# Start, first chunk and tail of a fused attention and convolution kernel: constant matmuls, a later spread, and another order of the last loads

## The chip, the cores and the metric

The kernel runs on one core of a Trainium2 chip. The time is device time in microseconds (us), median over several executions. A profile is one execution recorded by the hardware profiler; its span is the time from the first to the last recorded work. Engines are named as the profile names them: PE (TensorE, matmul), PEld (its weight load), DVE (VectorE), ACT (ScalarE), POOL (GpSimd) and SP (SyncE, which only starts transfers here). Each engine works through its own list of instructions in the order in which the program wrote them.

## What is computed

Two images, each of 256 channels and 64 x 64 pixels, all in float32, go through two layers.

Layer 0 is attention over all 4096 pixels of an image, with 8 heads of 32 channels, mixed with the input by a mask:

```python
attn = jax.nn.softmax(jnp.einsum('bnd,bmd->bnm', q, k), axis=-1)
fuse = jnp.einsum('bnm,bmd->bnd', attn, v)
hybrid = _conv1x1(jnp.concatenate([x, fuse], axis=1), Wf, bf)
return hybrid * m + x * (1.0 - m)
```

Layer 1 scales each channel by a gate made of two small matmuls, adds a second attention inside windows of 8 x 8 pixels (4 heads of 64 channels), shuffles the channels, runs two grouped 7 x 7 convolutions with normalisation between them, and returns the result times the sigmoid of the second convolution:

```python
y = lax.conv_general_dilated(x, sa_w1, (1, 1), [(3, 3), (3, 3)], dimension_numbers=dn, feature_group_count=cr)
y = jax.nn.relu(_bn(y + sa_b1))
y = lax.conv_general_dilated(y, sa_w2, (1, 1), [(3, 3), (3, 3)], dimension_numbers=dn, feature_group_count=cr)
return x * jax.nn.sigmoid(_bn(y + sa_b2))
```

## The kernel before

**Opening.** The pixels of an image are cut into 8 chunks of 512. For each of the 16 chunks of both images the kernel makes q and k (line 435, 16 matmul records to a chunk), then v (line 472), and writes them to memory outside the core. ACT starts the loads of the three weight matrices and then sixteen small loads of the biases `bq` and `bk` (lines 383 and 392) before its first arithmetic, the copy with bias at line 445. The squares of q and k go to DVE (line 454), whose maxima decide later between two versions of the attention; line 415 sums them by head on PE. The version that runs here is called `a`.

**Attention.** `pipeline` runs over 1024 slots: image `b`, chunk `c` of queries, half `g` of the heads (4 heads), block `m` of 128 keys. A chunk has 64 slots. In slot i, `scores(i + 2)` puts the score matmuls (line 633) on PE and three exponentials (line 643) on ACT, `products(i)` puts the value matmuls (line 662) on PE and, except at m = 0, one addition of 128 x 2048 elements on DVE (line 664), which sums the exponentials for the denominators. The exponentials lie in `EB = 8` buffers, so those of slot i + 8 can be written once the addition of slot i is done.

When a chunk's last slot is done, `at(delay, action)` puts actions into a list; an action runs at the end of the slot that is `delay` later. With `DN = 8`: after 8 slots the denominators are gathered on PE (line 685), after 9 DVE takes reciprocals (line 714), after 10 and 12 `spread` puts four matmuls each on PE (line 700) that spread the reciprocals over the channels, after 13 DVE multiplies the attention result `f` by them (line 717), and after 14 `stage(b, c)` is appended to the list of stages (line 1188).

A stage is everything of a chunk that follows its attention: the 1 x 1 convolution (line 732; first the half on `x`, then the half on `f`), the gate (lines 761 and 775), the window attention (lines 803 to 931) and its output projection (line 953). It is a generator cut into steps; every fourth slot runs one step (`run_stages`), so that its work lies among the slots of the next chunk. Its last step writes the chunk's rows, via `xo`, to the array `x_s` outside the core (line 979). Its first step also starts, on SP, the loads of the next chunk's `x` and mask (`load_x`, lines 573 and 576), which wait until this chunk's are no longer needed.

**Tail.** The convolutions start when the attention ends. They work on units of 4 groups of channels: 16 units, with both images wherever that is possible. `items` lists the work: the first `EARLY` units with image 0 alone, whose rows are complete; units 2 to `EARLY` - 1 with image 1 alone; the remaining units with both images; and last units 1 and 0 with image 1. `convolve` is a generator too. Its steps are `conv1(k + 1)` (line 1045), `conv2(k)` (line 1069) and `gate(k)` (lines 1091 and 1104, the last multiplication and the stores), and after each gate come the loads that the coming items need. These loads are started on SP, in program order with half of the stores: `load_rows` (line 1024) brings the pixels of item k + 4, `load_w` (line 1017) a unit's convolution weights of 896 KB. Weights of units other than 0 go into the 8 buffers that held exponentials. Two of them are loaded when the tail starts, one more after each gate.

While the last chunk's stage still runs, one step of `convolve` is placed after each of its larger steps. When it is done, `staged` is set; from then on `more()` makes the buffers for the rows of image 1 and loads the first four of them (`load_rows(EARLY + 3)`), which waits for the last chunk's rows to have arrived in `x_s`. The gates of the early items after that store through POOL alone.

Of the kernel before, what the change touches and what calls it, by code (L numbers as in the profile page):

```python
# [19 lines left out]
P = 128  # L20
# [9 lines left out]
AHEAD = 2  # L30
EB = 8
DN = 8
EARLY = 8
HEADS1, HD1 = 4, 64
WS = 8
NW = W // WS
# [19 lines left out]
def conv_seq_kernel(ctx: ExitStack, tc: tile.TileContext, a, out):  # L56
    nc = tc.nc
# [13 lines left out]
    def psum2(name):  # L71
        return ps["pair"].tile([P, 2, CH], F32, tag="s", name=name)

    def psum1(name):
        return ps["one"].tile([P, CH], F32, tag="h", name=name)
# [6 lines left out]
    ones = const.tile([P, P], F32, name="ones")  # L82
# [249 lines left out]
    def spread(row, n):  # L332
        f = row.shape[-1]
        return row.rearrange("p u f -> u p f").to_broadcast([NU, n, f])
# [37 lines left out]
    with (  # L372
# [38 lines left out]
        def norms(i, tops):  # L411
# [3 lines left out]
                nc.tensor.matmul(s_, headsum, tops[:, n, :], start=True, stop=True)  # L415
            nc.vector.tensor_reduce(nm[:, i : i + 1], s[:, 0 : CH // 4], AX.X, ALU.max)

        prepared = prepare(mk, cwp)
        next(prepared)
        for _ in range(3):  # L420
# [2 lines left out]
        for i, (b, c) in enumerate(chunks):  # L423
# [4 lines left out]
            for n, w in (("q", wq), ("k", wk)):  # L428
                s = psum2(f"{n}0_{b}_{c}")
                for g in range(KC):  # L430
                    for kc in range(KC):
                        rhs = x[:, kc, :]
                        if n == "q":
# [5 lines left out]
                            start=(kc == 0),  # L439
                            stop=(kc == KC - 1),  # L440
# [26 lines left out]
        for i, (b, c) in enumerate(chunks):  # L467
            s = psum2(f"v0_{b}_{c}")
            sv = s.rearrange("p a (t o) -> p (a t) o", t=2)
            for m in range(4):  # L470
                for kc in range(KC):
# [4 lines left out]
                        start=(kc == 0),  # L476
                        stop=(kc == KC - 1),
# [21 lines left out]
            elif i == 2:  # L499
# [3 lines left out]
                for oc in range(KC):  # L503
                    for kc in range(KC):
# [4 lines left out]
                            start=(kc == 0),  # L509
                            stop=(kc == KC - 1),  # L510
# [13 lines left out]
    def pipeline(arm, shifted, pools):  # L524
# [23 lines left out]
        stages = deque()  # L548

        def at(delay, action):  # L550
            later.append((now[0] + delay, action))
# [99 lines left out]
        def products(i):  # L651
            b, c, g, m = slots[i]
            if m == 0:
                acc[0] = avp.tile([P, CH], F32, tag="av", name=f"av{arm}_{i}")
                acc[1] = ep.tile([P, HG, CH], F32, tag="sum", name=f"sum{arm}_{i}", bufs=3)
                totals[b, c, g] = acc[1]
            av, total = acc[0], acc[1]
            e, v = es[i], vts[b, c, g, m // PB]
            start, stop = m == 0, m == NMB - 1
            for j in range(HG):  # L660
                r = slice(32 * j, 32 * j + 32)
                nc.tensor.matmul(av[r, :], v[:, m % PB, r], e[:, j, :], start=start, stop=stop)  # L662
            if m > 0:
                nc.vector.tensor_add(total, first[0] if m == 1 else total, e)  # L664
            e = es.pop(i)
            if start:
                first[0] = e
            if stop:
                if g == 0:
                    fts[b, c] = fp.tile([P, KC, CH], F32, tag="f", name=f"f{arm}_{b}_{c}")  # L670
                f = fts[b, c]
                nc.scalar.copy(f[:, g, :], av)  # L672
                if g == 0:
                    return
                both = [totals.pop((b, c, gg)) for gg in range(KC)]
                inv = fp.tile([P, P], F32, tag="inv", name=f"inv{arm}_{i}")
                rd = fp.tile([P, KC, 4, P], F32, tag="rd", name=f"rd{arm}_{i}")


                def denominators():  # L680
                    s = psum2(f"dn{arm}_{i}")
                    for h in range(HEADS0):
                        for q in range(4):
                            r = slice(32 * q, 32 * q + 32)
                            nc.tensor.matmul(  # L685
                                s[r, 0, 0:P],
                                keysum[:, h].rearrange("p i h -> p (i h)"),
                                both[h // HG][:, h % HG, q * P : (q + 1) * P],
                                start=(h == 0),
                                stop=(h == HEADS0 - 1),  # L690
                            )
                    nc.scalar.copy(inv, s[:, 0, 0:P])


                def spread(hh):
                    t = psum2(f"rd{arm}_{i}_{hh}")
                    for gg in range(KC):
                        for q in range(2):
                            r = slice(64 * hh + 32 * q, 64 * hh + 32 * q + 32)
                            nc.tensor.matmul(  # L700
                                t[:, q, gg * P : gg * P + P],
                                spread_h[r, gg].rearrange("p j d -> p (j d)"),
                                inv[r, :],
                                start=True,
                                stop=True,
                            )
                    nc.scalar.copy(
                        rd[:, :, 2 * hh : 2 * hh + 2, :],
                        t[:, :, 0 : KC * P].rearrange("p q (g n) -> p g q n", g=KC),
                    )  # L710


                at(DN, denominators)
                at(DN + 1, lambda: nc.vector.reciprocal(inv, inv))
                at(DN + 2, lambda: spread(0))
                at(DN + 4, lambda: spread(1))
                at(DN + 5, lambda: nc.vector.tensor_mul(f, f, rd.rearrange("p g q n -> p g (q n)")))

# [266 lines left out]

        items = [(u, (0,)) for u in range(EARLY)] + [(u, (1,)) for u in range(2, EARLY)]
        items += [(u, (0, 1)) for u in range(EARLY, NU)] + [(1, (1,)), (0, (1,))]
        staged = []  # L990

        def convolve():
# [12 lines left out]
            weights = deque([*range(1, NU), 1])  # L1005
            dst = out.rearrange("b (g i) r w -> b i r g w", i=4)

            def load_w(u):
                if u >= NU:
                    return  # L1010
                n = 2 * 32 * UW
                if u == 0:
                    t = cpool.tile([P, n], F32, name=f"w{arm}{u}")
                else:
                    t = ep.tile([P, HG, CH], F32, tag="e", name=f"w{arm}{u}")
                    t = t.rearrange("p h n -> p (h n)")[:, 0:n]
                nc.sync.dma_start(t, w_s[u])
                ws[u] = t

            def load_x(k):  # L1020
                u, images = items[k]
                x = xs[k] = early[k % 4] if k < EARLY else xcs[k % 4]
                for i, b in enumerate(images):
# [5 lines left out]
            def load_rows(k):  # L1029

                while len(xs) < min(k + 1, len(items)) and (
                    staged or B - 1 not in items[len(xs)][1]
                ):
                    load_x(len(xs))
# [53 lines left out]
            def gate(k, z):  # L1088
# [5 lines left out]
                if k == len(items) - 1:  # L1094
                    engines = (nc.scalar, nc.sync)
                elif staged and k < EARLY:
                    engines = (nc.gpsimd,)
# [12 lines left out]
            def more():  # L1110
                if staged and not xcs:
# [5 lines left out]
                    xcs.append(pool.tile([P, B * nb, UG, WP], F32, name=f"xl{arm}3"))  # L1117
                    load_rows(EARLY + 3)
                return bool(xcs)
# [2 lines left out]
            load_rows(3)  # L1122
            load_w(0)
            pool = yield
            for _ in range(2):
                load_w(weights.popleft())
            conv1(0)
            yield
            for k, (u, images) in enumerate(items):
                while len(xs) <= k + 1 < len(items):  # L1130
                    if not more():
                        yield
                conv1(k + 1)
                yield
                more()
                z = conv2(k)
                yield
                more()
                gate(k, z)
                if xcs or k + 4 < EARLY:  # L1140
                    load_rows(k + 4)

                if weights and (k < EARLY - 1 or k >= EARLY):
                    load_w(weights.popleft())

        def run_later():
# [23 lines left out]
        for i, (b, c, g, m) in enumerate(slots):  # L1170
            now[0] = i
            if (b, c, g, m) == (B - 1, NCHUNK - 1, 0, 0):
                for _ in banded:
                    pass
                conv = convolve()
                next(conv)
            if m % PB == 0:
                load_piece(i // PB + AHEAD)
            if g == KC - 1 and m == 0:
                nxt = (b, c + 1) if c + 1 < NCHUNK else (b + 1, 0)  # L1180
                if nxt[0] < B:
                    load_q(*nxt)
            rest = scores(i + 2) if i + 2 < len(slots) else None
            products(i)
            if rest:
                rest()
            if g == KC - 1 and m == NMB - 1:
                at(DN + 6, lambda b=b, c=c: stages.append(stage(b, c)))
            run_later()
            if i % 5 == 1:  # L1190
                next(banded, None)
            if i % 4 == 0:
                run_stages()
# [102 lines left out]
```

## Time and profile before

| | |
|---|---|
| three executions | 3018.35, 3022.46 and 3022.87 us; median 3022.46 us |
| profiled execution | 3021.93 us |
| its span | 3020.1 us |
| PE busy | 2970.8 us, 98% of the span |
| DVE busy | 2503.1 us, 83% |
| ACT busy | 2480.6 us, 82% |
| POOL busy | 267.1 us, 9% |
| opening, to the first score matmul | 0 to 187.4 us |
| attention, to the last value matmul | 187.4 to 2781.5 us |
| tail | 2781.5 to 3020.1 us |

The profile gives each engine's busy time, a timeline of instructions in order of time, the waits, and the chain of work that ended last, followed back from the last instruction. In the timeline a row has its start, its length, the engine, the line and the operation; rows that follow each other closely are merged, with their number behind an x. Brackets at the end say how long the engine had been idle before the row, and what ended that. "SPq", "ACTq" and "POOL ... DMA" rows are starts of transfers, not the transfers themselves. In the chain a row has its start, its length, and the engine and line or the transfer.

### The profile page before, as it was taken

What the parts mean: (1) busy time and instruction counts of PE and PEld (TensorE: products, weight loads), DVE (VectorE), ACT (ScalarE), POOL (GpSimd) and SP (SyncE); (2) the same over time, 40 slices, a digit from 0 to 9 for tenths busy, and PEclk for the clock granted to TensorE, in tenths of its full rate; (3) what the DMA queues carried; (4) which work ended last, traced back from release to release, by engine and by line L of the source; (5) the groups of instructions that cost most, each with busy time, mean ns of one, the idle gap of its engine ahead of it and who ended that gap; (6) DMA issues with size and microseconds to landing.
All of it is one profiled execution on the core that took longest, in us unless ns stands there. A gap on an engine that the chain in (4) does not pass through costs nothing.

```text
span 3020.1 us, 61026 instructions
## 1 busy us (share of the span) xinstructions
PE 2970.8 (98%) x25226; PEld 1017.2 (34%) x25226; DVE 2503.1 (83%) x1348; ACT 2480.6 (82%) x4151; POOL 267.1 (9%) x470
## 2 busy tenths in 40 slices
PE   9999899999999999999999999999999999999897
PEld 3552223223222222222223222323223222323585
DVE  3249989999999999998999999999999998998211
ACT  5569789898989898988989898989898998988333
POOL 8010000000000000000000000000000000000456
PEclk9999999999999999999999999999999999999998
DMA  8544322222142323232222222222323222321564
GB/s 243 196 174 160 107 69 66 69 65 70 52 80 63 79 62 73 66 73 68 67 68 64 71 58 67 62 73 62 80 59 69 71 71 67 104 60 54 163 196 104
DMA packets 224143, 266.03 MB, mean 88 GB/s; under 512 B 113576, under 2 KB 130300, under 8 KB 223600
## 3 DMA queue, kind: packets, MB, share of 16 engines
q1 hardware_dynamic: 200880, 231.47, 26.2%
q0 software_dynamic: 18416, 27.87, 4.4%
q8 instruction: 201, 3.29, 0.5%
q10 hardware_dynamic: 4560, 2.70, 0.3%
q14 instruction: 86, 0.70, 0.1%
HBM read 213.49 MB, written 66.13 MB: 93 GB/s over the span
## 4 chain that ended last, share of the span: by engine, by line
PE 92%; DVE 2%; DMA 2%; POOL 1%; ACT 1%; issue 1%; SPq 0%; ACTq 0%; DVEq 0%; POOLq 0%
PE sa L633 36%; PE ava L662 33%; PE hya L732 4%; PE qka L803 4%; PE vwa L889 2%; PE opa L953 2%; PE v L472 2%; PE q L435 2%; PE k L435 2%; DVE suma L664 1%; POOL out_dram L1104 1%; PE c1a L1045 1%; PE c2a L1069 1%; DMA out_dram<-za 1%; PE dna L685 1%
## 5 line engine op out<-in xcount | busy, mean ns | idle before, releaser
L664 DVE TENSOR_TENSOR suma<-suma,ea 128x2048 f32<-128x2048 f32 x960 | 2199.1, 2291 | 88.7 <-ACT ea L643 2.3
L643 ACT ACTIVATE ea<-sa 128x512 f32<-128x512 f32 (+1 forms) x3072 | 2044.8, 745 | 86.6 <-PE sa L633 39.3
L633 PE MATMUL sa<-qa,ka 32*128 32x512 f32 x8192 | 1191.4, 640 | 1.5 <-ACT vst L480 1.2
L662 PE MATMUL ava<-ea,va 128*32 128x512 f32 x8192 | 1091.6, 605 | 0.3 <-ACT fa L672 0.3
L633 PEld LDWEIGHTS sa<-qa,ka 32*128 32x128 f32 x8192 | 338.0, 183 | 755.4 <-ACT ea L643 688.3
L662 PEld LDWEIGHTS ava<-ea,va 128*32 128x32 f32 x8192 | 161.5, 108 | 779.7 <-issue 752.9
L979 POOL DMA_DIRECT2D xs<-xo x94 | 65.8, 708 | 2552.0 <-DVE xo L964 2551.8
L1104 POOL DMA_DIRECT2D out_dram<-za x210 | 117.9, 569 | 85.0 <-DVE za L1091 61.1
L803 PE MATMUL qka<-ua,qkv_w 128*128 128x512 f32 x256 | 118.4, 605 | 0.0
L664 DVE TENSOR_TENSOR suma<-ea,ea 128x2048 f32<-128x2048 f32 x32 | 73.1, 2284 | 51.3 <-ACT ea L643 51.3
L1091 DVE TENSOR_TENSOR za<-za,xla 128x768 f32<-128x768 f32 (+1 forms) x16 | 21.7, 1359 | 108.0 <-DMA out_dram<-za 57.9
L454 DVE TENSOR_REDUCE top<-sq 128x512 f32<-128x2048 f32 x16 | 36.6, 2286 | 81.3 <-ACT sq L448 81.3
L1069 PE MATMUL c2a<-yca,wa 32*128 32x192 f32 (+1 forms) x1344 | 98.1, 435 | 2.5 <-ACT za L1079 2.5
L740 ACT ACTIVATE ta<-hya,bf 128x512 f32<-128x512 f32 x32 | 20.2, 683 | 96.8 <-PE hya L732 96.8
L1079 ACT ACTIVATE za<-c2a 128x384 f32<-128x384 f32 (+1 forms) x48 | 26.1, 595 | 86.5 <-DMA out_dram<-za 61.4
L1069 PEld LDWEIGHTS c2a<-yca,wa 32*128 32x128 f32 x1344 | 89.6, 315 | 13.1 <-issue 9.8
L858 ACT ACTIVATE ewa<-ewa,mxwa 128x64 f32<-128x64 f32 x256 | 85.2, 346 | 1.5 <-DVE mxwa L849 1.5
L744 DVE TENSOR_TENSOR ta<-ta,mca 128x512 f32<-128x512 f32 x32 | 22.0, 689 | 67.6 <-ACT ta L740 67.6
L816 ACT ACTIVATE qka<-qka,qkv_b 128x512 f32<-128x512 f32 x64 | 40.4, 683 | 41.8 <-PE qka L803 41.6
L803 PEld LDWEIGHTS qka<-ua,qkv_w 128*128 128x128 f32 x256 | 46.0, 189 | 71.3 <-issue 46.1
L435 PE MATMUL q<-x,WqT 128*128 128x512 f32 x128 | 61.3, 624 | 5.6 <-DMA WqT<-in_WqT_dram 5.6
L889 PE MATMUL vwa<-qkv_w,ua 128*128 128x256 f32 x256 | 59.5, 386 | 0.0
(137 smaller groups left out, 1523.5 us busy)
## 6 DMA issues: line engine op xcount, KB each, us to landing
ka<-ks SPq DMA_DIRECT2D x256, 256.0 KB
va<-vs SPq DMA_DIRECT2D x256, 256.0 KB
wa<-ws SPq DMA_DIRECT2D x17, 896.0 KB
ws<-zeros SPq DMA_DIRECT2D x16, 896.0 KB
xs<-xo POOLq DMA_DIRECT2D x78, 140.0 KB, 5.8
xla<-xs SPq DMA_DIRECT2D x24, 420.0 KB
x<-in_x_dram SPq DMA_DIRECT2D x16, 512.0 KB
qs<-qst SPq DMA_DIRECT2D x16, 512.0 KB
```

The lines of the kernel that those rows point to most:

```text
L435: nc.tensor.matmul(s[:, g, :], w[:, kc, g * P : (g + 1) * P], rhs, start=(kc == 0), stop=(kc == KC - 1),)
L633: nc.tensor.matmul(heads[j], k[r, cols], q[r, g, :], start=True, stop=not shifted)
L643: nc.scalar.activation(e[:, h, :], tile, AF.Exp, scale=SCALE0)
L662: nc.tensor.matmul(av[r, :], v[:, m % PB, r], e[:, j, :], start=start, stop=stop)
L664: nc.vector.tensor_add(total, first[0] if m == 1 else total, e)
L732: nc.tensor.matmul(s[:, oc, :], wf[:, kc, oc * P : (oc + 1) * P], f[:, kc - KC, :] if half else xw[kc], start=(kc == 0), stop=(kc == 2 * K ...
L803: nc.tensor.matmul(s[:, j, :], wqkv[:, kc, o : o + P], u[:, kc, :], start=(kc == 0), stop=(kc == KC - 1),)
L858: nc.scalar.activation(e[:, n, :], e[:, n, :], AF.Exp, bias=mx[:, n : n + 1], accum_out=rs[:, n : n + 1],)
L889: nc.tensor.matmul(sv[:, t, :], u[:, kc, t * P : (t + 1) * P], wqkv[:, kc, 2 * C : 3 * C], start=(kc == 0), stop=(kc == KC - 1),)
L979: eng.dma_start(x_s[b, n, p + r0 : p + r1].rearrange("r g w -> g r w"), xo[64 * h : 64 * h + 64, oc, r0 - WS * c : r1 - WS * c, :],)
L1069: nc.tensor.matmul(tiles[j // 2][:, j % 2, 0 : n * W], w[r, d], y[r, 0:n, d : d + W], start=(d == 0), stop=(d == KS - 1),)
L1104: engines[stores % len(engines)].dma_start(dst[b, i, r0:r1, UG * u : UG * u + UG, :], z[p + r0 : p + r1, :, nb * m + n, :],)
```

## The change

Four edits.

1. Before the chunks' first matmuls, ten matmuls of a 128 x 128 tile of ones with itself, into a PSUM tile that nobody reads.
2. For the very first chunk alone, both spreads, the multiplication of `f` and the start of the stage come nine slots later than for the others (`late = EB + 1`). Denominators and reciprocals stay where they were.
3. Four units' weights are loaded when the tail starts, in place of two. After the gates, weights are loaded as long as the next unit is at most 9 (`1 + EB`), and then from item `EARLY` on. Before, one was loaded after each of the items 0 to 6 and from item 8 on.
4. `EARLY` is 7 in place of 8: unit 7 is done once for both images, not once for each. `items` has 23 entries where it had 24.

```diff
-EARLY = 8
+EARLY = 7
...
+        busy = psum1("busy")
+        for _ in range(10):
+            nc.tensor.matmul(busy[:, 0:P], ones, ones, start=True, stop=True)
...
+                late = EB + 1 if (b, c) == (0, 0) else 0
                 at(DN, denominators)
                 at(DN + 1, lambda: nc.vector.reciprocal(inv, inv))
-                at(DN + 2, lambda: spread(0))
-                at(DN + 4, lambda: spread(1))
-                at(DN + 5, lambda: nc.vector.tensor_mul(f, f, rd.rearrange("p g q n -> p g (q n)")))
+                at(DN + 2 + late, lambda: spread(0))
+                at(DN + 4 + late, lambda: spread(1))
+                at(DN + 5 + late, lambda: nc.vector.tensor_mul(f, f, rd.rearrange("p g q n -> p g (q n)")))
...
             pool = yield
-            for _ in range(2):
+            for _ in range(4):
                 load_w(weights.popleft())
...
-                if weights and (k < EARLY - 1 or k >= EARLY):
+                if weights and (weights[0] <= 1 + EB or k >= EARLY):
                     load_w(weights.popleft())
...
             if g == KC - 1 and m == NMB - 1:
-                at(DN + 6, lambda b=b, c=c: stages.append(stage(b, c)))
+                late = EB + 1 if (b, c) == (0, 0) else 0
+                at(DN + 6 + late, lambda b=b, c=c: stages.append(stage(b, c)))
```

## The prediction, made before the result was known

> **What bounds the kernel now.** I read the engine totals first, then the chain that ended last, then the timeline wherever the chain leaves PE.
>
> ```profile
> span 3020.1 us, 61026 instructions
> ...
> PE 2970.8 (98%) x25226; PEld 1017.2 (34%) x25226; DVE 2503.1 (83%) x1348; ACT 2480.6 (82%) x4151; POOL 267.1 (9%) x470
> ```
>
> PE is busy for all but 49.3 us of the span. A change that leaves the matmuls nearly alone can gain only from these 49 us and from matmuls run at half clock, so I look for the stretches where PE waits. In the chain, the opening:
>
> ```profile
> 1.80 8.02 DMA WvT<-in_WvT_dram
> 14.29 4.07 DMA bk<-in_bk_dram
> 21.15 2.30 DVE top L454
> 24.01 3.63 PE q L435 x8
> ```
>
> Up to 21 us the end is set by ACT's sixteen bias loads, their landing and ACT's first work, then by DVE; PE joins at 23.58 us. From there on PE runs on. The next long hole is in the first chunk's spread, in the timeline:
>
> ```profile
> 343.63 16.67 DVE L664 TENSOR_TENSOR suma<-suma,ea 128x2048 f32<-128x2048 f32 x7
> ...
> 360.21 0.94 DVE L714 RECIPROCAL inva<-inva 128x128 f32<-128x128 f32 x1
> ...
> 361.26 1.01 PE L700 MATMUL rda<-inva,spread_h 32*128 32x128 f32 x6 [8.99 <-issue]
> ...
> 385.72 1.14 PE L633 MATMUL sa<-qa,ka 32*128 32x512 f32 x8
> ```
>
> PE stood at the first spread (slot 73) for 8.99 us. The label names no releaser; the reciprocal ended at 361.15, so it is that. It was queued behind seven additions, 2.38 us each. Slots without a stage cost PE 2.07 us but DVE 2.39, so by the end of chunk 0 PE is a full ring of eight buffers ahead. The last line is the first slot after `hya`, the reference point below. In the tail, PE's part of the timeline and SP's:
>
> ```profile
> 2814.86 2.53 PE L1045 MATMUL c1a<-xea,wa 128*32 128x192 f32 x56 [1.24 <-DMA wa<-ws]
> ...
> 2839.46 4.19 PE L1045 MATMUL c1a<-xea,wa 128*32 128x192 f32 x56 [1.84 <-DMA wa<-ws]
> ...
> 2866.15 4.62 PE L1045 MATMUL c1a<-xea,wa 128*32 128x192 f32 x56 [9.38 <-DMA wa<-ws]
> ```
>
> ```profile
> 2848.76 1.33 SPq L979 DMA_DIRECT2D xs<-xo  x2
> 2856.16 2.01 SPq L1024 DMA_DIRECT2D xla<-xs  x4
> 2858.22 1.54 SPq L1017 DMA_DIRECT2D wa<-ws  x3
> ```
>
> Three waits for weights (units 3, 5, 7), and two of those convolutions took 4.2 and 4.6 us where the others take 2.54. Unit 7's load stood on SP behind four row loads, which waited for the last chunk's rows to be written out.
>
> **What the Trainium skill says.** "TensorE: Matmul & The Clock Gate", Part 1: the clock falls to half after an idle window of about 3.4 us and returns after about as long a busy one; the windows run freely. The trace agrees: 0.50 granted from 2862 to 2870, and idle times of 1.84 us and more were followed by it, 1.24 us was not. Its first table says VectorE's queue is strictly first in, first out: the reciprocal's wait above shows it. "DMA: Bandwidth & Descriptors", Anatomy of one DMA: about 2 us fixed besides the bytes. Here 420 KB of rows and 896 KB of weights, started together at 2808.80, landed at 2814.82; at the 383 GB/s seen from 2812 to 2814 the bytes take 3.5 us, which leaves 2.5. The same page, Queues, rings and completion order: each DMA engine takes descriptors in ring order, so a load queued first lands about first. No single row landing shows in the trace.
>
> **Edit 1, ten constant matmuls: 0.** Twenty records (float32 makes two of each). Before, the first `q` records at half clock stood 0.86 us apart, the later ones 0.43, so PE may reach full speed 2.3 us sooner. Nobody is waiting for it: ACT starts bias loads until 15.2 us and its first copy ran at 16.52, when `q` had ended at 11.4; the fourth group waits for PSUM until 17.8 in any case; DVE's maxima, which PE needs at 23.58, do not move. From the other side: the weight load seen at half clock is 0.34 us, a 128-column matmul by the rows above 0.21; at their sum, 0.55, for all twenty records the matmuls end 11 us after 1.2, at 12.2, and four groups of 3.45 then end at 26.0, 2.4 us too late. If the clock rises after some 4.4 us, as it did before, they end near 8 and the groups at 22. I take 0, range 0 to -2.4.
>
> **Edit 2, the later spread: +3.5.** The spreads move from slots 73 and 75 to 82 and 84, the multiplication of `f` from 76 to 85, the stage's first step from 80 to 88. The 8.99 us go: at slot 82 the reciprocal is long done. What is late next is `f`. Without PE's stop DVE never catches up: after the reciprocal, 361.15, it has slots 73 to 85 to add, 13 x 2.385 = 31.0, then 1.22 for `f`: 393.4. PE reaches slot 88 sooner: its exponentials need the addition of slot 80, 361.15 + 8 x 2.385 = 380.2; with 2.0 of ACT and the matmuls about 385; the half of `hya` on `x` takes 3.6, to 388.6. There PE waits 4.8 us, with everything behind it, for `f`. `hya` ends at 393.4 + 3.6 = 397.0, or 398.9 if the clock drops. Before, it ended at 385.7 with slots 81 to 88 still to do, 8 x 2.067 = 16.5: 402.2. Gain 5.2 or 3.4; a 4.8 us stop should drop the clock, so 3.5. Moved with the first step: the copies of line 740 and DVE's lines 744 and 746, then SP's loads of the next `x` and mask. DVE gives `x1` at 393.4 + 3 x 2.39 + 2.8 = 403.4, and PE wants it at slot 92, 397 + 8.3 = 405.3 or later: hidden by 2 us. SP stands at those loads until then; behind them is the piece of keys for slots 100 to 103, not needed for another 10 us, and the next chunk's stage wants its `x` some 120 us later. Bounds: 2 to 6.
>
> **Edit 3, weights earlier: +10.8 net.** Units 3 and 4 start behind units 1 and 2 on SP, when additions 1018 and 1019 end (about 2772 and 2775); SP's next instruction is at 2805, so nothing queues. Weights now come one item further ahead, plus one: unit 5 starts after gate 0 for the convolution at 2839, unit 6 after gate 1, and unit 7 has 12 items of time. Removed: 1.24 at 2814.86; at 2839.46 the convolution can start at 2837.6 and end at 2840.1, so the output projection (line 953), whose own input from ACT comes at 2839.46, starts at 2840.1, not 2843.58: 3.5. Together 4.7. At 2866.15, 9.38 of wait and 4.62 - 2.54 = 2.08 of clock: 11.5. In their place: the item there is now unit 2 of image 1, which needs rows. Those are written 4.7 earlier, landing at 2855.97 - 4.7 = 2851.3; unit 8's weights, 2.3 us of bytes, now start 1.4 us before that write, so I add an estimated 0.7: 2852. The first row load is ahead of three others; 2.2 to 2.5 us fixed and 1.1 of bytes give 2855.5. PE is there at 2856.78 - 4.7 = 2852.1: a wait of 3.4, and 2.0 for the clock. Net 4.7 + 11.5 - 5.4 = 10.8. Bounds: no wait, 16.2; if the four loads share the queue (1.72 MB, 4.4 us) and the write is 2 us late, the wait is 8 and the net 6.
>
> **Edit 4, unit 7 once: +2.3.** Two single items (5.97 us each from start to start) become one double (9.63). POOL's stores for the early items fall from 48 to 36; the double's 24, over two queues at 0.56, are 6.7 us under 9.6 of PE. The row load after gate 3 goes.
>
> **Sum.** 0 + 3.5 + 10.8 + 2.3 = 16.6 off the profiled 3021.93 is 3005.3. That execution is 0.5 below the median; from the median, 3005.9. I say 3005.5.
>
> **Rivals.**
> *The rows take the weights' place in full* (0.14): a wait of 10 us where I have 3.4, so 3012. For it: writing the rows took 6.2 us and SP waited 5.7 for it. Against: loads ahead in the ring land first.
> *The first chunk gains nothing* (0.11): PE's wait is passed on as lag of DVE, at `f`, then at `x1` with only 2 us of margin: 3009. For it: DVE needs 151.3 of each later chunk's 162.8 us, so lag drains slowly. Against: that is still 11.5 of slack a chunk.
> *Slower, by the same rows* (0.04): they land after 2879, when the wait has eaten the 16.6 and 6 more: each further microsecond costs one, and 30 us of landing gives 3028. Against: the longest landing in the tail was 7.8.
> *The edits do not act* (0.05): unit 7's wait moves whole onto the rows, edits 2 and 4 yield nothing, and only the first 4.7 are left: 3018.
>
> **From chances to numbers.** My own case has 0.64; 0.02 is left for slower ways I do not see. A measurement here can tell 0.2%, 6 us: faster means under 3016.4, slower over 3028.5. My case and two rivals are faster, 0.89; 0.05 same; 0.06 slower. The range goes from 3000, with no wait for rows (5.4 more), to 3013, the first rival.
>
> **What would show it.** Right: no `wa<-ws` wait on PE in the tail; a wait of 2 to 5 us at the first `xla` convolution; no hole near 352, but one of 4 to 5 us inside the first `hya`, near 390; PE's first norm matmul still at 23.6; 23 items. Wrong: the row wait far from 3.4 us, PE waits at `x1` or `u` in chunk 1, or the norm matmul later than 24.

## The result, and the profile after

The changed kernel takes 3005.42 us (median; 3004.22 to 3006.27), the kernel before, run on the same occasion, 3022.66 us (3018.35 to 3024.31). The ratio is 0.9945, with a 95% interval of 0.9929 to 0.9960: faster by 0.55%, or 17 us. The profiled execution took 3006.27 us with a span of 3004.5; the one before took 3021.93 with a span of 3020.1. What follows explains the 15.6 us between these two spans.

The engine totals of the changed kernel:

```profile
PE 2972.6 (99%) x25134; PEld 1016.6 (34%) x25134; DVE 2502.3 (83%) x1347; ACT 2479.8 (83%) x4147; POOL 263.8 (9%) x464
```

PE is idle for 3004.5 - 2972.6 = 31.9 us, where it was 49.3. That is 17.4 less idle time for 15.6 less span: PE's busy time has grown by 1.8 (the constant matmuls alone add 4.6). The gain is idle time removed.

To place the gain I cut both spans at the first score matmul and at the first matmul of the tail (`c1a`), both of which the PE timeline shows.

| us | before | after | difference |
|---|---|---|---|
| opening, to the first score matmul | 187.40 | 188.93 | +1.5 |
| attention, from there to the first `c1a` | 2593.4 | 2590.2 | -3.2 |
| tail, from the first `c1a` to the end | 239.3 | 225.4 | -13.9 |
| span | 3020.1 | 3004.5 | -15.6 |

**Opening.** PE's timeline of the kernel before, then of the changed kernel:

```profile
23.58 0.42 PE L415 MATMUL nrm<-top,headsum 128*32 128x128 f32 x8 [1.73 <-DVE top L454]
23.94 3.70 PE L435 MATMUL q<-x,WqT 128*128 128x512 f32 x8
```

```profile
1.14 4.64 PE L421 MATMUL busy<-ones 128*128 128x128 f32 x20 [1.14 <-POOL ones L83]
...
23.41 0.43 PE L415 MATMUL nrm<-top,headsum 128*32 128x128 f32 x8 [2.04 <-DVE top L459]
23.76 5.40 PE L440 MATMUL q<-x,WqT 128*128 128x512 f32 x8
```

The constants ended at 5.8 us, and the first norm matmul started at 23.41, where it was 23.58 before. So they delayed nothing there. But behind the norm the third chunk's `q` took 5.40 us where it was 3.70. One of the profile's windows of this stretch gives the reason. It lists the stretch and its length; then, with the number of instructions in brackets, the busy time of PE, PEld, DVE, ACT and POOL; then the granted clock, here 0.52 of full speed; and last the share and the GB/s of the DMA engines:

```profile
24.00:26.00 2.00, 2.00 (x3) 0.72 (x3) 0.00 (x0) 1.97 (x4) 0.51 (x1) 0.52 1.10 330
```

The clock stood at half. The extra 1.5 us sit here.

**First chunk.** DVE's timeline, then PE's, of the changed kernel:

```profile
361.73 0.95 DVE L722 RECIPROCAL inva<-inva 128x128 f32<-128x128 f32 x1
362.60 30.98 DVE L669 TENSOR_TENSOR suma<-suma,ea 128x2048 f32<-128x2048 f32 x13
393.49 1.22 DVE L725 TENSOR_TENSOR fa<-fa,rda 128x1024 f32<-128x1024 f32 x1
```

```profile
372.41 0.71 PE L705 MATMUL rda<-inva,spread_h 32*128 32x128 f32 x8
...
394.77 6.05 PE L740 MATMUL hya<-fa,WfT 128*128 128x512 f32 x8 [4.29 <-DVE fa L725]
```

The 8.99 us at the first spread are gone: its row has no bracket. Thirteen additions now stand between the reciprocal and `f`, 31 us without a gap, and PE waits 4.29 us for `f`. The half of `hya` behind the wait takes 6.05 us, not 3.6: half clock again.

**Tail.** PE's timeline, then SP's, of the changed kernel:

```profile
2834.53 2.54 PE L1053 MATMUL c1a<-xea,wa 128*32 128x192 f32 x56
2836.99 3.70 PE L961 MATMUL opa<-ota,out_w 128*128 128x512 f32 x8
...
2853.35 4.19 PE L1053 MATMUL c1a<-xla,wa 128*32 128x192 f32 x56 [3.19 <-DMA xla<-xs]
2857.47 3.58 PE L1077 MATMUL c2a<-yca,wa 32*128 32x192 f32 x56
```

```profile
2842.17 1.33 SPq L987 DMA_DIRECT2D xs<-xo  x2
...
2849.82 1.99 SPq L1032 DMA_DIRECT2D xla<-xs  x4
```

None of the tail's convolutions waits for weights any more. Where one had waited 9.38 us for `wa`, one now waits 3.19 us for `xla`, the first rows of image 1. SP could start their load at 2849.82, once the last chunk's rows had been written; it landed 3.5 us later, with PE's start at 2853.35. This convolution, too, runs at half clock: 4.19 us where 2.54 is usual.

### The profile page after: what moved, and what is told of

Read it like the earlier page. It is cut to its first block, busy times and chain, and to the rows that moved or that the text cites. A ratio compares the mean times of both kernels' runs of the same rounds, so it can differ in the third digit from the quotient of the medians.

```text
span 3004.5 us, 60832 instructions
## 1 busy us (share of the span) xinstructions
PE 2972.6 (99%) x25134; PEld 1016.6 (34%) x25134; DVE 2502.3 (83%) x1347; ACT 2479.8 (83%) x4147; POOL 263.8 (9%) x464
## 4 chain that ended last, share of the span: by engine, by line
PE 90%; DVE 4%; DMA 2%; ACT 1%; POOL 1%; SPq 1%; issue 0%; ACTq 0%; DVEq 0%
PE sa L638 35%; PE ava L667 33%; PE qka L811 4%; PE hya L740 4%; DVE suma L669 3%; PE vwa L897 2%; PE opa L961 2%; PE q L440 2%; PE v L477 2%; PE k L440 2%; DMA out_dram<-za 1%; POOL out_dram L1112 1%; PE dna L690 1%; PE sca L845 1%; DVE za L1099 1%; PE c2a L1077 1%
## 5 line engine op out<-in xcount | busy, mean ns | idle before, releaser
L1099 DVE TENSOR_TENSOR za<-za,xla 128x1536 f32<-128x1536 f32 (+1 forms) x16 | 22.5, 1409 | 110.8 <-ACT za L1093 56.9
L1053 PE MATMUL c1a<-xla,wa 128*32 128x384 f32 (+1 forms) x896 | 62.8, 431 | 3.2 <-DMA xla<-xs 3.2
L740 PE MATMUL hya<-fa,WfT 128*128 128x512 f32 x128 | 60.0, 613 | 4.3 <-DVE fa L725 4.3
```

Of the source, the lines that this page charges most:

```text
L740: nc.tensor.matmul(s[:, oc, :], wf[:, kc, oc * P : (oc + 1) * P], f[:, kc - KC, :] if half else xw[kc], start=(kc == 0), stop=(kc == 2 * K ...
L1053: nc.tensor.matmul(s[32 * j : 32 * j + 32, 0 : n * W], w[:, j, d, :], xs[k][:, 0:n, j, d : d + W], start=(d == 0), stop=(d == KS - 1),)
```

## The experiments

Each kernel was run against the kernel before on the same chip. First the four edits one by one (edit 1 also the other way round, and edit 2 in a second size), then what the tail showed, then two versions that put the findings together. The ratio is over several executions; the three columns to its right are in microseconds and come from one profile of each kernel.

| kernel | ratio to before (95%) | first score | attention | tail |
|---|---|---|---|---|
| before | 1 | 187.4 | 2593.4 | 239.3 |
| the change | 0.9945 (0.9929 to 0.9960) | 188.9 | 2590.2 | 225.4 |
| e1_constants_only | 1.0002 (0.9993 to 1.0010) | 187.2 | 2594.3 | 238.2 |
| a5_no_constants | 0.9945 (0.9931 to 0.9958) | 187.2 | 2589.5 | 225.5 |
| e2_later_spread_only | 0.9985 (0.9979 to 0.9992) | 187.2 | 2590.8 | 238.4 |
| a7_spread_four_later | 0.9935 (0.9921 to 0.9948) | 188.8 | 2585.7 | 227.8 |
| e3_weights_only | 0.9959 (0.9945 to 0.9973) | 187.1 | 2593.6 | 227.5 |
| e4_seven_units_only | 0.9969 (0.9956 to 0.9981) | 187.4 | 2593.9 | 230.6 |
| e5_weights_only_stores_shared | 0.9981 (0.9975 to 0.9988) | 187.4 | 2593.3 | 234.6 |
| e6_weights_only_three_z | 0.9943 (0.9930 to 0.9957) | 187.1 | 2593.8 | 222.3 |
| a6_second_convolution_first | 0.9944 (0.9930 to 0.9957) | 187.8 | 2589.6 | 226.5 |
| b1_seven_units_swapped | 0.9909 (0.9894 to 0.9924) | 187.1 | 2585.6 | 221.0 |
| b2_eight_units_four_ahead | 0.9911 (0.9896 to 0.9926) | 187.4 | 2586.0 | 222.2 |

### Edit 1: the constants alone, and the change without them

```diff
+        busy = psum1("busy")
+        for _ in range(10):
+            nc.tensor.matmul(busy[:, 0:P], ones, ones, start=True, stop=True)
```

> The kernel before with edit 1 alone. Theory: the constants finish q and k sooner, PE then idles longer before the first norm matmul (2.04 us where it was 1.73), the clock drops to half there and the third chunk's q takes 5.3 us, not 3.6: the first score matmul comes 1.5 us later (188.9, not 187.4) and the time is +1.5. Rival: that drop was chance and edit 1 does nothing: first score matmul at 187.4, time 0.

Measured: 3023.17 us against 3022.49. PE's timeline of this kernel at the same place:

```profile
23.29 0.43 PE L415 MATMUL nrm<-top,headsum 128*32 128x128 f32 x8 [2.04 <-DVE top L458]
23.65 3.70 PE L439 MATMUL q<-x,WqT 128*128 128x512 f32 x8
```

The constants make PE wait a little longer for the norm here too: 2.04 us as in the changed kernel, 1.73 in the one before. Yet `q` behind it takes 3.70, at full clock. So the longer stop alone does not make the clock fall; the first score matmul comes at 187.16, where it was 187.40 before.

The same from the other side, the change with edit 1 taken out:

```diff
-        busy = psum1("busy")
-        for _ in range(10):
-            nc.tensor.matmul(busy[:, 0:P], ones, ones, start=True, stop=True)
```

> The changed kernel without edit 1. If edit 1 costs 1.5 us by itself: first score matmul at 187.3, not 188.9, and -1.5. If edit 1 does nothing, as it did alone, and the half clock in the third chunk's q was one execution's: also about 187.3 here, and no difference in time to be measured, 0.

Measured: 3005.74 us, ratio 0.9945, the same as the whole change. Its profile has no half clock after the norm, and its first score matmul comes at 187.18. Four profiles in all have edit 1, and in all four PE stands 2.04 or 2.05 us before the first norm; half clock follows in one. The nine without it have stops of 1.05 to 1.73 us and no half clock. Two other profiles with edit 1 start their attention late (187.82 and 188.82), for another reason: PE's norm matmul in the fourth chunk waits 0.47 and 1.59 us, because ACT stands 4.9 and 6.4 us at its own loads of `ca_w` and `ca_b`. So three of the four profiles with edit 1 start 0.4 to 1.5 us later than any of the nine without it (187.07 to 187.42). That is a pattern in few profiles; no run here shows whether the constants cause it. In time, edit 1 is worth nothing that can be measured: alone, its interval runs from 2.1 us faster to 3.0 us slower.

### Edit 2: the later spread alone, and four slots in place of nine

```diff
+                late = EB + 1 if (b, c) == (0, 0) else 0
-                at(DN + 2, lambda: spread(0))
+                at(DN + 2 + late, lambda: spread(0))
...
-                at(DN + 6, lambda b=b, c=c: stages.append(stage(b, c)))
+                at(DN + 6 + late, lambda b=b, c=c: stages.append(stage(b, c)))
```

> The kernel before with edit 2 alone. Theory: the 9.0 us hole at the first spread goes, a wait of 4 to 5 us for f inside the first hya comes, with about 2.4 us of half clock behind it; the end of the attention comes 3.2 us sooner and so does the end: -3.2. Rival: the wait at f and later lag of DVE give all of it back: 0.

Measured: 3018.27 us against 3022.49; the interval of the ratio is 2.4 to 6.3 us of gain. The span is 3.7 us shorter, of which the attention gives 2.6. The half of `hya` on `f` waits 4.28 us and takes 6.64. So the stop at `f` is the same as in the changed kernel, and edit 2 acts by itself.

If what PE lacks at `f` is DVE's time, an earlier spread should spread the stop out. The change with four slots in place of nine:

```diff
-                late = EB + 1 if (b, c) == (0, 0) else 0
+                late = 4 if (b, c) == (0, 0) else 0
```

> The changed kernel with the first chunk's spreads, f and stage 4 slots later, not 9. Theory: f is multiplied at slot 80 and the stage starts at 84; the spread waits 1.6 us for the reciprocal, f is done when hya wants it, no half clock: against the changed kernel -2.8. Rival: the wait at the first spread comes back in full size (5 us and a half clock) and takes the gain: 0 or slower.

Measured: 3003.16 us; the attention takes 2585.7, which is 4.5 less than with nine slots and 7.7 less than before. PE's timeline of this kernel:

```profile
362.70 0.60 PE L705 MATMUL rda<-inva,spread_h 32*128 32x128 f32 x6 [0.73 <-ACT ea L648]
...
382.70 3.70 PE L740 MATMUL hya<-fa,WfT 128*128 128x512 f32 x8 [0.76 <-DVE fa L725]
...
414.79 3.70 PE L811 MATMUL qka<-ua,qkv_w 128*128 128x512 f32 x8 [1.44 <-DVE ua L801]
```

As a whole this kernel's ratio, 0.9935, cannot be told from the change's 0.9945; the difference is seen in the stage, and two kernels further down with four slots have the same attention (2585.6 and 2586.0), where the four kernels with nine have 2589.5 to 2590.8. The one stop of 4.29 us has become three, 0.73, 0.76 and 1.44, and after none of them do the matmuls run at half clock: `hya` takes 3.70. That is 4.29 + 2.45 - 2.93 = 3.8 us of the 4.5. The stage comes earlier, so `f` stands behind fewer additions; and part of the lag is then met at `ua`, further on. The tail of this profile is 2.4 us longer than the changed kernel's, with a wait of 4.3 for the rows, which is why the whole gains less than the attention does.

### Edits 3 and 4: each alone

Weights alone, with eight early units as before:

```diff
-            for _ in range(2):
+            for _ in range(4):
                 load_w(weights.popleft())
...
-                if weights and (k < EARLY - 1 or k >= EARLY):
+                if weights and (weights[0] <= 1 + EB or k >= EARLY):
```

> The kernel before with edit 3 alone, 8 units of image 0. Theory: all three weight waits go (4.7 and 11.5 us with their clock), and unit 7 of image 0 still lies between PE and the first rows of image 1, which then have 6 us more to land: no wait in their place, -16.2, more than edits 3 and 4 gave together in the tail (-13.9). Rival: the rows' round trip takes over here too: a wait of 3 us or more at the first xla convolution, -11.

Measured: 3010.69 us against 3022.49, 12 us less. Neither a wait for weights nor one for rows is left at the first convolutions of the tail. PE's timeline shows another wait:

```profile
2882.40 4.25 PE L1069 MATMUL c2a<-yca,wa 32*128 32x192 f32 x52 [2.16 <-ACT za L1079]
2886.57 3.02 PE L1045 MATMUL c1a<-xla,wa 128*32 128x192 f32 x56
```

The second convolution waits for `za`, ACT's copy of an earlier one: 2.16 us here, after 0.37 nine microseconds earlier, and two convolutions are slowed by the clock (4.25 for 3.57, 3.02 for 2.54). That is 3.7 us which the changed kernel does not have, and most of what is missing to 16. ACT's own timeline tells what ACT waits for:

```profile
2881.86 0.87 ACT L1079 ACTIVATE za<-c2a 128x384 f32<-128x384 f32 x2 [6.85 <-DMA out_dram<-za]
```

The copy goes into one of two buffers, and that buffer's content had not been stored yet. The starts of such stores, in POOL's timeline:

```profile
2848.92 10.05 POOL L1104 DMA_DIRECT2D out_dram<-za  x18 [3.41 <-DVE za L1091]
```

With eight early units POOL alone starts 48 stores, 0.56 us each: 6.7 us for the twelve of an item, where PE takes 6.0 for the item. Before, PE's 9.38 us of waiting for weights had given POOL time for them. For the copy at 2881.86 the trace lets this be counted: DVE had filled the buffer before by 2868.55, and POOL, still at the stores of earlier items, reached the last of its twelve at about 2878, an estimate from the number of starts; the landing took the rest. My reading is that POOL is what is late next, once that wait is gone; two more runs below put it to the test.

Seven units alone:

```diff
-EARLY = 8
+EARLY = 7
```

> The kernel before with edit 4 alone, weights two ahead as before. Theory: the waits of 1.2 and 1.8 us for units 3 and 5 stay; the 9.4 us wait for unit 7 goes, since unit 7 is no longer due there, and a wait of about 3 us for rows with 1.7 us of clock comes; 2.3 us for the merged unit: 11.5 - 4.7 + 2.3 = -9.1. Rival: the 9.4 us hang on the order of the weight loads, whichever unit is due: only the merged unit is gained, -2.3.

Measured: 3013.85 us against 3022.49, 9 us less, about as expected. PE's timeline:

```profile
2839.60 3.75 PE L1045 MATMUL c1a<-xea,wa 128*32 128x192 f32 x56 [2.12 <-DMA wa<-ws]
...
2860.44 4.09 PE L1045 MATMUL c1a<-xla,wa 128*32 128x192 f32 x56 [3.58 <-DMA xla<-xs]
```

The waits for units 3 and 5 are still there (0.62 and 2.12), but the one of 9.38 has gone without edit 3: with seven early units the item at that place needs rows, not unit 7's weights. It waits 3.58 us for them. The tails of the two kernels are 11.8 and 8.7 us shorter than before, 20.5 together; the two edits in one kernel give 13.9. Both remove the same 9.38 us, and they cannot remove it twice.

### What stands behind the tail of edit 3

Two ways to take POOL's stores off the path, both on the kernel with edit 3 alone. The first shares the early stores between POOL and ACT:

```diff
-                    engines = (nc.gpsimd,)
+                    engines = (nc.gpsimd, nc.scalar)
```

> Edit 3 alone as before, and the stores of the image 0 items that follow the last stage start on POOL and ACT in turn, not on POOL alone. Theory: with edit 3 alone the waits of 5 us at the second convolutions, and the half clock after them, came from POOL, which had 48 stores at 0.57 us to start while PE went on at 6 us an item; shared, they go, and the full 16.2 us against the kernel before appear. Rival: the waits come from the stores' landing or from elsewhere: they stay, and the gain stays at 12.

Measured: 3017.84 us against 3023.55, slower than with edit 3 alone. The timeline of ACT's queue, then PE's:

```profile
2848.67 10.68 ACTq L1104 DMA_DIRECT2D out_dram<-za  x6
```

```profile
2859.87 4.28 PE L1045 MATMUL c1a<-xea,wa 128*32 128x192 f32 x56 [8.04 <-ACT yca L1053]
```

ACT stood 10.68 us at the starts of six stores, and with it the copy `yca` that PE's next convolution needed. The starts themselves last 0.3 to 0.6 us each; the rest is four gaps between them, of 0.7 to 4.0 us. The next three groups of six starts on ACT took 2.5 us each. The waits for `za` have shrunk to 0.3 us, but a wait of 8.04 has come in their place. Since that wait also gives POOL time, the run settles nothing about POOL. What ACT waited for in the gaps of the first group stays open.

The second leaves the stores on POOL and gives the copies a third buffer:

```diff
-                z = pool.tile([P, 4, B * nb * W], F32, tag="z", name=f"z{arm}{k}", bufs=2)
+                z = pool.tile([P, 4, B * nb * W], F32, tag="z", name=f"z{arm}{k}", bufs=3)
```

> Edit 3 alone, with three buffers for the product of the gate where there were two. Theory: POOL starts stores at 6.9 us an item while PE goes on at 6.0, and the lag reaches PE through the two buffers; one buffer more takes it up: no waits at the second convolutions, -16.2 against the kernel before. Rival: something else holds them, waits of 5 us and a half clock stay: -12.

Measured: 3005.47 us against 3023.12; the span is 16.9 us shorter than before, the tail 17.0. PE's waits in this tail (waiting engine and output, what it waits for; sum in us, number, longest):

```profile
PE c1a L1045 <- DMA xla<-xs: 1.5, 1, 1.5
...
PE c2a L1069 <- ACT za L1079: 0.2, 1, 0.2
```

In the kernel with edit 3 alone the row for `za` was:

```profile
PE c2a L1069 <- ACT za L1079: 5.1, 3, 2.5
```

The number of stores and their queues are the same in both kernels; only the buffer differs. So the stores reached PE through the two `z` buffers. But not all of the 17.0 us belongs to edit 3. Of the 5.1, 2.5 stood near the end of the tail, between the last two second convolutions, where the kernel before has such a wait too, and the changed kernel one of 2.39. PE's timeline there, before and with three buffers:

```profile
3002.21 4.40 PE L1069 MATMUL c2a<-yca,wa 32*128 32x192 f32 x52 [2.51 <-ACT za L1079]
```

```profile
2981.77 7.71 PE L1069 MATMUL c2a<-yca,wa 32*128 32x192 f32 x112
```

With three buffers the two run as one row, without a stop. From the start of the first of them to the end of the span it is 24.4 us before, 23.6 with edit 3 alone and 21.4 here; the ten kernels with two buffers have 23.6 to 26.0, the three with three 20.8 to 21.8. So 3.0 of the 17.0 us are gained at the end, where every kernel with a third buffer is shorter, whatever its other edits. Up to there edit 3 gains 11.1 us with two buffers and 14.0 with three, not the full 16: a wait of 1.5 for later rows has come in. No run has the third buffer as its only edit.

### The wait for rows in the changed kernel

PE's 3.19 us for `xla` come ahead of the first convolution on image 1. The second convolution of the item before it has its data by then, and takes 3.6 us. On the changed kernel, that one first:

```diff
+                swap = k == EARLY - 1
+                if not swap:
+                    conv1(k + 1)
+                    yield
...
+                if swap:
+                    conv1(k + 1)
+                    yield
```

> The changed kernel, with the second convolution of the last image 0 item ahead of the first convolution on rows of image 1. Theory: PE has 3.5 us of work while the rows land: the wait of 3.2 us and the 1.65 us of half clock go, against the changed kernel -4 to -4.8. Rival: POOL's 36 stores then hold PE up as they did with edit 3 alone, waits at the second convolutions appear, and 3 us or more are given back: -1.5 at most.

Measured: 3005.73 us, no gain. PE's timeline, then ACT's:

```profile
2854.24 2.54 PE L1053 MATMUL c1a<-xla,wa 128*32 128x192 f32 x56 [1.63 <-DMA xla<-xs]
...
2858.73 4.19 PE L1053 MATMUL c1a<-xla,wa 128*32 128x192 f32 x56 [1.96 <-ACT yca L1061]
```

```profile
2856.62 0.87 ACT L1087 ACTIVATE za<-c2a 128x384 f32<-128x384 f32 x2 [6.37 <-DMA out_dram<-za]
...
2858.27 0.41 ACT L1061 ACTIVATE yca<-c1a,cbias 128x192 f32<-128x192 f32 x1
```

The wait for rows is shorter, 1.63, and full clock follows it. But the second convolution's copy comes earlier too and waits for its `z` buffer until 2856.62. ACT's copy `yca` is queued behind it, the next first convolution waits 1.96 us for that, and the half clock is paid there. The stop has moved on by one item.

### Two versions put together

The swap needs the third buffer, as edit 3 does. The change without edit 1, with four slots, the swap and three buffers:

```diff
-        busy = psum1("busy")
...
+                late = 4 if (b, c) == (0, 0) else 0
...
-                z = pool.tile([P, 4, B * nb * W], F32, tag="z", name=f"z{arm}{k}", bufs=2)
+                z = pool.tile([P, 4, B * nb * W], F32, tag="z", name=f"z{arm}{k}", bufs=3)
...
+                swap = k == EARLY - 1
```

> The changed kernel without edit 1, with the spread four slots later in place of nine, the second convolution of the last image 0 item ahead of the first one on image 1's rows, and three gate buffers. Theory: attention 7.7 us sooner than before, tail 13.9 + 4.8 sooner: 2996 to 2998. Rival: the second half of the swap's gain is lost again, as with two buffers, since rows still come 1.6 us late and the clock halves: 3001.

Measured: 2995.57 us against 3023.12. PE's timeline at the place of the row wait:

```profile
2840.18 7.72 PE L1073 MATMUL c2a<-yca,wa 32*128 32x192 f32 x112
2848.06 2.54 PE L1049 MATMUL c1a<-xla,wa 128*32 128x192 f32 x56 [0.15 <-DMA xla<-xs]
2851.14 2.55 PE L1049 MATMUL c1a<-xla,wa 128*32 128x192 f32 x56 [0.54 <-ACT yca L1057]
```

Two second convolutions run back to back ahead of the rows; the wait for rows is 0.15, the one for `yca` 0.54, and no convolution here is at half clock. Against the kernel before, the attention is 7.8 us shorter and the tail 18.3. The 18.3 lie near the expected 18.7 by luck: against the changed kernel the tail is 4.4 us shorter, but only 1.7 of them come before the last two second convolutions (a later row load makes PE wait another 1.31), and 2.7 come from the end, where the third buffer acts and the expectation had nothing.

The other version has eight early units and no swap: the kernel before with edit 3, four slots and three buffers.

```diff
+                late = 4 if (b, c) == (0, 0) else 0
...
-                z = pool.tile([P, 4, B * nb * W], F32, tag="z", name=f"z{arm}{k}", bufs=2)
+                z = pool.tile([P, 4, B * nb * W], F32, tag="z", name=f"z{arm}{k}", bufs=3)
...
-            for _ in range(2):
+            for _ in range(4):
```

> The kernel before with edit 3, the spread four slots later and three gate buffers; no constants, eight units of image 0. Theory: attention 7.7 us sooner, tail 16.2: 2998.6, and close to the swapped one with seven units. Rival: the eighth unit's 48 stores on POOL still hold PE: 3003.

Measured: 2996.52 us. The rival is not quite gone: PE still waits 1.93 us for `za` at one convolution, and the end is 3.6 us shorter than before, as in the other two kernels with a third buffer. The ratios of the two, 0.9909 and 0.9911, cannot be told apart. By their ratios both beat the changed kernel's 0.9945 by some 10 us, and the intervals do not overlap. Neither has edit 1, and the second has no edit 4 either.

## Why the prediction was right, point by point

The predicted median was 3005.5 us and the measured one is 3005.42. That they agree to 0.1 us is luck: the executions spread over 2 us, and the sum was 16.6 us off the profiled execution where 15.6 came off the span. What carries the prediction is its terms. From the two profiles:

| term | predicted | measured |
|---|---|---|
| edit 1, opening | 0 (range 0 to -2.4) | -1.5 |
| edit 2, first chunk | +3.5 | +3.2 |
| first two waits for weights | +4.7 | +4.9 |
| third wait, less the wait for rows | +6.1 | +6.6 |
| unit 7 once, and the rest of the tail | +2.3 | +2.4 |
| sum | 16.6 | 15.6 |

The tail's terms are measured after taking off the 1.7 us by which it starts earlier (2780.79 to 2779.09). The output projection started at 2843.58 and now starts at 2836.99: 6.6 less 1.7 is 4.9. The second convolution behind the large wait moved from 2870.70 to 2857.47: 13.2, less 1.7 and 4.9, is 6.6. What is left of 13.9 is 2.4, a remainder and not a measurement of the merged unit by itself.

**Edit 1** was the one term that missed, within its range and by a way that the prediction had not priced. The step "Nobody is waiting for it ... I take 0" held: the norm matmul came at 23.41, predicted 23.6. The constants ended earlier than the estimate, at 5.8, not near 8: twenty records took 4.64 us, 0.23 each, where it had priced one at 0.55. (That the first `q` before ran at half clock is read from durations, 0.86 for 0.43; the granted clock in the windows from 4 to 12 us reads 1.00.) But `q` and `k` then ended sooner, so that PE stood 2.04 us before the norm, not 1.73, and in this profile half clock followed: 1.5 us to the first score. The prediction had looked for a loss in late matmuls and not in a longer stop. Over the runs nothing stands against the 0: the constants alone measure 1.0002, and the change has 0.9945 with and without them.

**Edit 2** went as worked out. The step "PE waits 4.8 us, with everything behind it, for `f`" measured 4.29. Everything came 1.3 to 1.9 us later, with the opening: `f` ended at 394.7, predicted 393.4, and PE was there at 390.5, predicted 388.6. DVE's part came as computed, 31.0 us for thirteen additions and 1.22 for the product. The wait was followed by half clock, as "a 4.8 us stop should drop the clock" had it; it cost 6.05 - 3.60 = 2.45 us, predicted 1.9 (the three other kernels with nine slots have 1.8 twice and 3.0). The margin at `x1` held: PE waits neither there nor at `ua` in the changed kernel. The rival in which lag eats the gain was wrong for nine slots, but the mechanism in it is real: with four slots PE meets the lag at `ua`, 1.44 us, and loses less in all. The nine slots are not the best choice for the attention, which the prediction did not ask.

**Edits 3 and 4** went as worked out together. The row load started at 2849.82, which is 2851.5 on the clock of before (1.7 added), predicted 2852; it took 3.5 us, predicted 2.2 to 2.5 and 1.1; PE waited 3.19, predicted 3.4; the clock cost 4.19 - 2.54 = 1.65, predicted 2.0. That the first of the row loads is ahead in its queue is what bounded the wait, as the argument against the first rival had it. The Trainium skill ("DMA: Bandwidth & Descriptors", Queues, rings and completion order) says only that descriptors are taken in ring order, and warns that loads need not complete in that order; that the first one lands first is the prediction's own step. Here the measurement bears it out: a landing 3.5 us after the start while three more row loads stood behind, where the prediction's bound for a shared queue had 4.4 us of bytes alone. The fixed 2 us that the prediction took from the same page stand there in a section on transfers that POOL starts; these loads are SP's, and what the sum rests on is the 2.5 us read from the trace.

Two parts of the bookkeeping were wrong without moving the sum. First, the whole of the 9.38 us was booked on edit 3 and only 2.3 on edit 4, but edit 4 alone also removes it (measured 9 us). The waits belong to places, and an edit alone need not be worth its row in the sum. Second, POOL's stores were called covered because the double item hides them. That holds for the changed kernel with its 36 early stores; with 48, edit 3 alone loses 3.7 us to them, clock included, and three buffers give 3.0 of it back before the end. The cover was thinner than the text let on: the swap, which only brings one copy forward, falls through it.

The last rival, that edits do not act, is excluded for edits 2, 3 and 4 by their own runs, and describes edit 1. The rival with late rows would have needed a row wait of 10 us; the longest seen in any of these kernels at that place is 4.3. One figure of the slower rival does not come out: counted from 2852, rows that land after 30 us are 26.5 us later than 2855.5, which gives 3032, not 3028.

## What to carry to other kernels

When an engine that is behind makes another one wait, moving the consumer moves the wait, and its new size is simple addition: the queue in order, up to the piece that is needed next. Choose the place so that the lag is met in several short stops, because here, apart from the first microseconds of the program, a stop of 1.8 to 5 us was mostly followed by half clock, worth another 0.8 to 3.0 us, while stops up to 1.73 us never were. Before a large wait is removed, ask which engine was using it to catch up (here POOL, through two buffers), and do not add up two edits that remove the same wait. And when a combination meets its sum, check stage by stage that the gain lies where the sum put it: a third buffer, added for one place, paid at another.

## What the runs showed of the hardware that was not expected

- What follows a stop of about 2 us is not settled by its length: four profiles have the same 2.04 to 2.05 us before the norm matmul, and the clock fell after one of them. The freely running windows that the Trainium skill describes ("TensorE: Matmul & The Clock Gate", Part 1) would explain such chance, but no run here shows them. Its idle window of about 3.4 us is longer than these stops, and longer than those of 1.84, 1.96 and 2.12 us that were followed by slow convolutions here (4.19, 4.19 and 3.75 us for 2.54). So the prediction's "The trace agrees" holds for the half clock, not for the length of the window; there the measured stops decide.
- Six starts of stores on ACT were spread over 10.68 us, though each lasted 0.3 to 0.6; the next three groups of six took 2.5 us each. POOL was starting stores in all four stretches, so that alone is not the reason. No run here tells what is.
